# An earlier opening, rows of two, three and three sequences, and halved vector pieces in a two-layer gated attention kernel

## The chip, the cores and the metric

The kernel runs on one core of one Trainium2 chip. The metric is the device time of one execution in microseconds (us). The kernel before the change took 2823.27 us (median of 3 runs, 2820.88 to 2829.08).

## What is computed

The reference updates x (8 sequences of 512 tokens, 256 channels) four times, with a second input ctx (8 x 512 x 128) and a tanh gate before each update:

```python
x = x + tanh(g_xattn[0]) * L0_xattn(layernorm(x), ctx)   # 16 heads of 16: causal self plus cross attention
x = x + tanh(g_ffn[0])   * L0_ffn(layernorm(x))          # both linears on integers, scales taken over all of x
x = x + tanh(g_xattn[1]) * L1_xattn(layernorm(x), ctx)   # block a1 (self), then block a2 (cross), each attention + MLP
x = x + tanh(g_ffn[1])   * L1_ffn(layernorm(x))          # ternary linear, depthwise conv of 3, SiLU, ternary linear
```

The two scales of L0_ffn need the minimum and maximum over all sequences, so nothing behind them can start before the last sequence has passed. In layer 1 the blocks are per sequence: block a2 of a sequence needs the output of block a1 of the same sequence, and L1_ffn needs that of a2.

## The kernel before, in words

All work is cut into steps, and a planner in Python writes them out in one order when the program is built. The class `Pace` keeps, for each engine, the time at which it would be free, and for each tile the time at which it would be done. A step is a generator that stops at `need(...)` (L915), which names the tiles it waits for and whether its next instruction goes to TensorE. `weave_timed` (L1057) orders layer 0, `weave_all` (L1791) orders layer 1. Each picks, among the steps that could start within 0.3 us of TensorE's next free moment, the one with the lowest place in the plan: a stream's `base` plus its `share` of progress, against the index of the next attention step. A step that doesn't use TensorE is written out as soon as its tiles are ready. Streams with a `lag` (the lists of first and last jobs: 1.0) also wait until VectorE's planned queue is at most that long (L1808). The engines run what was written in that order, each waiting only for its data.

**Layer 0, opening (L1174).** The first sequence's normalisation (`norm0`), its transposes and self values (`pre0`), and its first query and key projections (`pairs0(0, 0, 0)`) are written alone, before the attention steps begin. PSUM has one bank (`m1`) for them, so each transpose group, each pair of value tiles and each projection waits until the one before has been copied out. The scores have three two-bank buffers (`st`), which are empty then. An attention step has a front (scores, exp on ScalarE, for self attention a causal mask on GpSimd) and a back (probabilities times values); a back is written one front later (`end_rest`).

**Layer 1 (L1757).** The order of the attentions is written by hand: slots 0 to 15, each one sequence and one block. The sequences go in rows of two: (0, a1), (1, a1), (0, a2), (1, a2), (2, a1), (3, a1), and so on. For every slot k there is a stream of projections (`pair1`), and one for each half of the MLP (`mlp1`, base k + 1). The MLP of block a1 goes on into `enter1`, which normalises twice and writes `zT`, from which the queries of the same sequence's a2 block are projected. The MLP weights are held for one block at a time and reloaded when a row ends. `first(b)`, the second linear of L0_ffn for sequence b, feeds block a1 of that sequence; `last(b)` is all of L1_ffn for it. These fifteen jobs stand in one list, `few`, sorted by base and worked off strictly one behind the other; `tail` does L1_ffn for sequence 7.

In `first`, each half of a sequence is one ScalarE operation and two VectorE operations over 2048 columns (L1912 to L1916). In `last`, each half has a maximum over 2048 columns (L2298), a product (L2313) and a rounding (L2315). The load of the a2 values into `vt` stands inside `mlp1` (L2109).

Of the kernel before, what the change touches and what calls it, by code (L numbers as in the profile page):

```python
# [25 lines left out]
MAGIC = 12582912.0  # L26
NEG = -1.0e30
PTS = 3
KEYS_FIRST = 6
# [884 lines left out]

def need(*tiles, pe=True, room=()):  # L915


    return [Pace.name(t) for t in tiles], pe, room

# [29 lines left out]
class Fast(General):  # L949
# [114 lines left out]
    def weave_timed(self, ops, streams, drain=False):  # L1064
# [17 lines left out]
        def starts(s):  # L1082
            names, on_pe, room = s.need
            t = max([pace.when(names)] + [pace.place(tag) for tag in room])
            return max(t, pace.place("m1")) if on_pe else t
# [73 lines left out]
    def layer0_xattn(self, w8pool):  # L1159
# [4 lines left out]
        with (  # L1164
# [8 lines left out]
            self.load0(wpool)  # L1173
            self.weave_timed([], [Stream(self.chain(self.norm0(0), self.pre0(0), self.pairs0(0, 0, 0)), 1.0)])  # L1174
            for b in range(B):
                streams = [Stream(self.pairs0(b, 1), 7.0, 0.88)]
                if b:
                    streams.append(Stream(self.post0(b - 1), 4.0, 0.88))
                else:
                    streams.insert(0, Stream(self.cross0(0), 5.0, 2.0))  # L1180
                if 1 <= b <= 4:
# [162 lines left out]
    def pre0(self, b):  # L1344
# [24 lines left out]

    def pairs0(self, b, u, *which):  # L1370

        work, q = self.work, self.seqs[b]

        while u and (0, 1) not in q:
            yield WAIT
        for s in which or (0, 1):
            src = (q["xnT"], q["ctxT"])[s]
            yield need(q["xnT"])
            ps = self.proj(self.wqk[("wq", "wcq")[s]], q["xnT"], u * P)
# [3 lines left out]
            ps = self.proj(self.wqk[("wk", "wck")[s]], src, u * P)  # L1383
            KT = [work.tile([P, T], F32, tag="KT", name="KT", bufs=8) for _ in range(2)]
            for e in range(2):
                self.out_of(KT[e], ps, self.par[:, e : e + 1], self.kbe[:, s, u, e : e + 1])
            q[u, s] = (QT, KT)

    def steps0(self, b, u):
# [7 lines left out]
        def front_at(e, s):  # L1397
            if (u, s) not in q or ("v", s) not in q:
                return 1e9
# [3 lines left out]
        def front(e, s, kt):  # L1403
# [9 lines left out]
            if s == 0:  # L1413
# [4 lines left out]
                )  # L1418
            reads = [Pace.name(pt), Pace.name(q["v", s])]
            self.coming = (reads, kt == 0, lambda: back(e, s, kt, lo, pt))  # L1420

# [35 lines left out]
        def rest_at():  # L1457
            if self.rest is None:
                return 0.0
            names, opens, _ = self.rest  # L1460
            t = pace.when(names)
# [275 lines left out]
    def layer1_xattn(self):  # L1737
        nc, tc = self.nc, self.tc
        with (
# [18 lines left out]
            self.li1s, self.mlps, self.loads, self.both_in = [0, 0], [0, 0], {}, {}  # L1758
            order = [(2 * p + k, blk) for p in range(B // 2) for blk in range(2) for k in range(2)]
# [16 lines left out]
            for half in range(2):  # L1776
                mlps[half][-1].base += 0.4 * half
                mlps[half].append(Stream(self.tail(half), 20.0, 1.0, 17 + 0.4 * half))
            self.final, self.tails = {}, [0, 0]
# [3 lines left out]
            self.weave_all(  # L1783
                [self.steps1(b, blk) for b, blk in order], [few, pairs, *mlps, *pres, diag, keys]
            )
# [5 lines left out]
    def weave_all(self, attns, chains):  # L1791
# [60 lines left out]
    def weight(self, name, b, blk):  # L1852

        while self.loads.get(name) != self.slot_of(b, blk) // 2:
# [30 lines left out]
    def first(self, b):  # L1885
# [142 lines left out]
    def slot_of(self, b, blk):  # L2028

        return 4 * (b // 2) + 2 * blk + b % 2  # L2030

# [8 lines left out]
    def pair1(self, b, blk, g):  # L2040
# [16 lines left out]
        q["QK", blk, g] = (QT, KT)  # L2057
        self.pairs += 1

    def mlp1(self, b, blk, half):  # L2060
# [38 lines left out]
        if blk:  # L2099
# [3 lines left out]
            nc.vector.scalar_tensor_tensor(res, res, self.gate[:, 1:2], x, ALU.mult, ALU.add)  # L2103
        elif not half:
            while self.nvt < self.slot_of(b, 1) or self.backs < 16 * (self.slot_of(b, 1) - 1):
                yield WAIT
            vt = q["vt", 1] = work.tile([P, NT, 2 * C], F32, tag="vt", name="vt", bufs=2)
            self.nvt += 1
            nc.sync.dma_start(vt.rearrange("p t c -> p (t c)"), self.vd[b])  # L2109
        li2 = yield from self.weight("li2", b, blk)  # L2110
# [133 lines left out]
    def last(self, b):  # L2244
# [25 lines left out]
        for half in range(2):  # L2270
# [3 lines left out]
            for f in range(NF):  # L2274
# [18 lines left out]
            yield need(h, pe=False)  # L2293
            nc.scalar.activation(h, h, AF.Silu)
            yield need(h, pe=False)

            hm = work.tile([P, n], F32, tag="hm", name="hm")
            nc.vector.tensor_reduce(  # L2298
                hm, h.rearrange("p f t -> p t f"), AX.X, ALU.max, apply_absolute_value=True
            )  # L2300
            yield need(hm)
# [9 lines left out]
            nc.scalar.copy(sr, self.row_of(sc, range(2)))  # L2311
            yield need(sr, pe=False)
            nc.vector.tensor_tensor(h, h, sr.unsqueeze(1).to_broadcast([P, NF, n]), ALU.mult)  # L2313
            hq = work.tile([P, NF, n], BF16, tag="hq", name="hq")
            nc.vector.tensor_scalar(hq, h, MAGIC, MAGIC, ALU.add, ALU.subtract)  # L2315
            nc.vector.tensor_scalar(k, un, self.units["f1_w2"], self.gate[:, 3:4], ALU.mult, ALU.mult)
# [238 lines left out]
```

## Time and profile before

| what | value |
|---|---|
| median of 3 runs | 2823.27 us |
| the profiled execution | 2823.82 us, span 2822.1 us |
| TensorE busy | 2520.0 us, 89% |
| VectorE, ScalarE, GpSimd busy | 61%, 51%, 22% |
| mean granted TensorE clock | 0.956 |
| first scores of layer 0 | 30.70 us |
| end of layer 0's attentions, about | 720 us |
| last instruction of layer 1's slots 0, 5, 10, 15 (copy of the last head group) | 1014.0, 1562.6, 2105.8, 2667.7 us |

A slot of layer 1 takes some 110 us: (2667.7 - 1014.0) / 15. PE is TensorE, PEld its weight loads, DVE VectorE, ACT ScalarE, POOL GpSimd. "PEclk" is the TensorE clock that was granted, as a share of full speed. In a timeline the columns are start, duration, engine, line, operation, output and input, and in brackets the idle time before it with what ended it. In a table of windows each engine has its busy time and, in brackets, its instructions; behind them stand the granted clock, the DMA share and GB/s.

### The profile page before, as it was taken

What the parts mean: (1) busy time and instruction counts of PE and PEld (TensorE: products, weight loads), DVE (VectorE), ACT (ScalarE), POOL (GpSimd) and SP (SyncE); (2) the same over time, 40 slices, a digit from 0 to 9 for tenths busy, and PEclk for the clock granted to TensorE, in tenths of its full rate; (3) what the DMA queues carried; (4) which work ended last, traced back from release to release, by engine and by line L of the source; (5) the groups of instructions that cost most, each with busy time, mean ns of one, the idle gap of its engine ahead of it and who ended that gap; (6) DMA issues with size and microseconds to landing.
All of it is one profiled execution on the core that took longest, in us unless ns stands there. A gap on an engine that the chain in (4) does not pass through costs nothing.

```text
span 2822.1 us, 38446 instructions
## 1 busy us (share of the span) xinstructions
PE 2520.0 (89%) x15452; PEld 1222.3 (43%) x15452; DVE 1725.1 (61%) x3072; ACT 1448.3 (51%) x1785; POOL 615.0 (22%) x682
## 2 busy tenths in 40 slices
PE   6999999999675888999999998999999999898875
PEld 2333333333232334535554445456354455354454
DVE  4544544343475555575657767766767755768766
ACT  4666675666573444445445534454555454555431
POOL 2112222111101343231422121232223112212010
PEclk9999999999897989999999999999999999999988
DMA  3001110010364411312210120131120020121010
GB/s 111 22 29 49 49 64 27 12 34 12 116 272 178 154 45 64 113 64 75 72 53 23 45 90 24 59 131 50 53 90 31 28 78 23 31 83 46 15 45 16
DMA packets 77339, 181.79 MB, mean 64 GB/s; under 512 B 7520, under 2 KB 36576, under 8 KB 69344
## 3 DMA queue, kind: packets, MB, share of 16 engines
q1 hardware_dynamic: 74768, 176.05, 17.9%
q8 instruction: 123, 2.02, 0.3%
q0 software_dynamic: 800, 2.62, 0.3%
q10 hardware_dynamic: 1584, 0.58, 0.1%
q14 instruction: 64, 0.52, 0.1%
HBM read 116.32 MB, written 62.91 MB: 64 GB/s over the span
## 4 chain that ended last, share of the span: by engine, by line
PE 69%; DVE 17%; ACT 7%; issue 3%; POOL 3%; DMA 1%; ACTq 0%; POOLq 0%; DVEq 0%
PE ps L1050 39%; PE ps_s L1050 16%; PE ov L1050 12%; DVE hext L1665 2%; PE ps L1053 2%; POOL dg L2179 1%; ACT pt L1412 1%; ACT pt L2175 1%; DVE hF L2290 1%; DVE hm L2298 1%; DVE acc L2204 1%; DVE mv L1936 1%; DVE acc L2206 1%; DVE rb L2222 1%; ACT hD L2122 1%
## 5 line engine op out<-in xcount | busy, mean ns | idle before, releaser
L2175 ACT ACTIVATE pt<-ps_s 128x1024 f32<-128x1024 f32 x512 | 496.3, 1021 | 443.5 <-PE ps_s L1050 357.1
L1050 PE MATMUL ps_s<-QT,KT 32*128 32x512 f32 (+3 forms) x4096 | 613.2, 610 | 29.0 <-ACT pt L2175 12.6
L1412 ACT ACTIVATE pt<-ps_s 128x1024 f32<-128x1024 f32 (+3 forms) x512 | 411.2, 862 | 197.4 <-PE ps_s L1050 190.9
L1050 PEld LDWEIGHTS ps_s<-QT,KT 32*128 32x128 f32 x4096 | 192.5, 185 | 365.2 <-issue 204.4
L2179 POOL TENSOR_SCALAR_AFFINE_SELECT dg<-pt 128x512 f32<-128x512 f32 x128 | 123.2, 964 | 651.6 <-ACT pt L2175 651.5
L1050 PE MATMUL ps<-li,hD 128*128 128x256 f32 x1024 | 238.8, 389 | 12.1 <-ACT hD L2122 12.1
L1050 PE MATMUL ps<-x3T,li 128*128 128x256 f32 x1024 | 244.0, 390 | 1.4 <-ACT x3T L2092 1.1
L1050 PE MATMUL ov<-pt,v 128*32 128x512 f32 (+3 forms) x2048 | 232.7, 525 | 13.9 <-POOL pt L1415 12.5
L1050 PE MATMUL ov<-pt,vt 128*32 128x512 f32 (+3 forms) x1792 | 204.9, 524 | 39.4 <-DVE oT L2224 33.2
L1050 PEld LDWEIGHTS ps<-li,hD 128*128 128x128 f32 x1024 | 193.4, 193 | 66.2 <-issue 17.6
L1050 PEld LDWEIGHTS ps<-x3T,li 128*128 128x128 f32 x1024 | 192.1, 194 | 55.3 <-issue 15.3
L1415 POOL TENSOR_SCALAR_AFFINE_SELECT pt<-pt 128x512 f32<-128x512 f32 x128 | 87.0, 681 | 477.4 <-ACT pt L1412 477.4
L1942 POOL TENSOR_SCALAR mv<-mv 128x2 f32<-128x2 f32 (+1 forms) x105 | 49.8, 475 | 630.8 <-DVE mv L1937 589.8
L2206 DVE TENSOR_TENSOR acc<-acc,pt 128x2048 f32<-128x2048 f32 x64 | 151.4, 2366 | 8.2 <-ACT pt L2175 7.2
L2204 DVE TENSOR_TENSOR acc<-pt 128x2048 f32<-128x2048 f32 x64 | 149.9, 2342 | 0.6 <-ACT pt L2175 0.6
L1437 DVE STREAM_TRANSPOSE ot<-ov 128x512 f32<-128x512 f32 x64 | 45.8, 716 | 156.3 <-PE ov L1050 156.3
L1050 PE MATMUL ps<-zT,a_wq 128*128 128x512 f32 x256 | 131.7, 640 | 6.1 <-DVE zT L2023 4.1
L2290 DVE SCALAR_TENSOR_TENSOR hF<-hp,cols,hF 128x256 f32<-128x256 f32 x224 | 113.1, 505 | 34.6 <-ACT hF L2281 28.1
L1050 PE MATMUL ps<-li,oT 128*128 128x256 f32 x512 | 128.0, 394 | 1.6 <-DVE oT L2224 1.1
L1050 PEld LDWEIGHTS ps<-li,oT 128*128 128x128 f32 x512 | 94.0, 193 | 44.5 <-issue 16.4
L1050 PEld LDWEIGHTS ov<-pt,v 128*32 128x32 f32 x2048 | 40.5, 107 | 168.0 <-issue 102.2
L1729 ACT ACTIVATE hD<-ps,cols 128x256 f32<-128x256 f32 x121 | 53.7, 472 | 108.8 <-PE ps L1050 72.9
(293 smaller groups left out, 3624.1 us busy)
## 6 DMA issues: line engine op xcount, KB each, us to landing
hd<-h SPq DMA_DIRECT2D x16, 1024.0 KB, 3.9
hF<-hd SPq DMA_DIRECT2D x16, 1024.0 KB, 6.7
li<-in_w_a_dram SPq DMA_DIRECT2D x16, 1024.0 KB, 5.0
fw<-q_f_w SPq DMA_DIRECT2D x22, 512.0 KB, 6.0
xF<-xd SPq DMA_DIRECT2D x22, 512.0 KB, 4.5
kd<-k SPq DMA_DIRECT2D x8, 1024.0 KB, 5.6
vd<-v SPq DMA_DIRECT2D x8, 1024.0 KB, 5.3
res<-rd SPq DMA_DIRECT2D x32, 256.0 KB, 2.7
```

The lines of the kernel that those rows point to most:

```text
L1050: self.nc.tensor.matmul(out, lhsT, rhs, start=start, stop=stop, skip_group_check=True)
L1053: self.nc.tensor.transpose(out, in_, self.ident)
L1412: nc.scalar.activation(pt[:, 2 * jp : 2 * jp + 2, lo:], pss[jp][:, :, lo:], AF.Exp)
L1415: nc.gpsimd.affine_select(out=diag, in_=diag, compare_op=ALU.is_ge, fill=0.0, base=0, pattern=[[0, 4], [1, P]], channel_multiplier=-1,)
L1665: nc.vector.tensor_reduce(e, hh, AX.X, op)
L1729: self.nc.scalar.activation(out, ps, AF.Identity, bias=bias)
L1942: nc.gpsimd.tensor_scalar(rstd, mv[:, :, 1], EPS, None, ALU.add)
L2175: nc.scalar.activation(pt[:, 2 * jp : 2 * jp + 2, :], pss[jp], AF.Exp)
L2179: nc.gpsimd.affine_select(out=dg, in_=pt[:, :, diag], compare_op=ALU.is_gt, fill=0.0, base=0, pattern=[[0, 4], [-1, P]], channel_multiplier=1,
L2204: nc.vector.tensor_tensor(st["acc"], st["pt"], pt, ALU.add)
L2206: nc.vector.tensor_tensor(st["acc"], st["acc"], pt, ALU.add)
L2290: nc.vector.scalar_tensor_tensor(a, hp[:, half + k : half + k + n], self.col("conv_w", 3 * f + k), a, ALU.mult, ALU.add)
```

## The change

**Opening.** `opening0` takes the place of `pre0` for the first sequence. Its eight transposes go into the two banks of one score buffer without a copy between them; ScalarE copies one bank out and VectorE the other. Query and key projections then use the two banks of a second score buffer. The self values come no longer before the first scores but as the head of the stream that holds the cross values, woven among the attention steps. A front needs no values any more, only a back does.

**Rows.** The attentions of layer 1 go in rows of two, three and three sequences. Slots 0 to 3 stay; then come (2, a1), (3, a1), (4, a1), (2, a2), (3, a2), (4, a2), (5, a1), (6, a1), (7, a1), (5, a2), (6, a2), (7, a2). The bases of the first and last jobs change with it, and the load of the a2 values gets a stream of its own. Weights are reloaded at five row ends instead of seven.

**Pieces.** The operations over 2048 columns in `first`, and the maximum, product and rounding in `last`, are cut in two, with a stop of the planner between them. A step can now name ScalarE as the engine whose queue its lag refers to.

```diff
+ROWS = ((0, 1), (2, 3, 4), (5, 6, 7))
+FIRST_AT = (-1, 0, 1, 2, 4, 5, 7, 9)
+LAST_AT = (6, 7, 8, 11, 12, 13, 15)
...
-            self.weave_timed([], [Stream(self.chain(self.norm0(0), self.pre0(0), self.pairs0(0, 0, 0)), 1.0)])
+            self.weave_timed([], [Stream(self.chain(self.norm0(0), self.opening0()), 1.0)])
...
-                    streams.insert(0, Stream(self.cross0(0), 5.0, 2.0))
+                    values = self.values0(0, 0, self.seqs[0]["xnT"], self.wv0["wv"], "bv")
+                    streams.insert(0, Stream(self.chain(values, self.cross0(0)), 12.0, 1.2))
...
+    def opening0(self):
+        q = self.seqs[0]
+        xnT = q["xnT"] = self.work.tile([P, 2, T], F32, tag="xnT", name="xnT", bufs=1)
+        yield need(q["z"], pe=False)
+        ps = self.st.tile([P, 2, T], F32, tag="st", name="ps_s")
+        for c in range(2):
+            for i in range(NT):
+                self.tp(ps[:, c, i * P : (i + 1) * P], q["z"][:, i, c * P : (c + 1) * P])
+        self.nc.scalar.copy(xnT[:, 0, :], ps[:, 0, :])
+        self.nc.vector.tensor_copy(xnT[:, 1, :], ps[:, 1, :])
+        yield from self.pairs0(0, 0, 0, two=True)
...
+            banks = self.st.tile([P, 2, T], F32, tag="st", name="ps_s") if two else None
+            ps = self.proj(self.wqk[("wq", "wcq")[s]], q["xnT"], u * P, ps=two and banks[:, 0, :] or None)
...
-            if (u, s) not in q or ("v", s) not in q:
+            if (u, s) not in q:
...
-            for k, b in zip((-1, 0, 1, 2, 3, 4, 7, 8), range(B)):
+            for k, b in zip(FIRST_AT, range(B)):
...
-            for k, b in zip((5, 6, 9, 10, 13, 14, 15), range(B - 1)):
+            for k, b in zip(LAST_AT, range(B - 1)):
...
-            names, on_pe, _ = s.need
-            t = max(pace.when(names), pace.free["DVE"] - s.lag)
+            names, on_pe, _, on = s.need
+            t = max(pace.when(names), pace.free[on] - s.lag)
...
-        if self.both(b, (name, blk)) and b % 2 and (b, blk) != (B - 1, 1):
+        if self.both(b, (name, blk)) and b == self.rows[self.row_at(b, blk)][1][-1] and (b, blk) != (B - 1, 1):
...
-            yield need(h, pe=False)
-            nc.scalar.activation(h, h, AF.Identity, scale=self.rh, bias=self.magic)
-            yield need(h, pe=False)
-            nc.vector.tensor_scalar(h, h, self.hlo, self.hhi, ALU.max, ALU.min)
+            for f in (slice(0, NF // 2), slice(NF // 2, NF)):
+                yield need(h, pe=False, on="Activation")
+                nc.scalar.activation(h[:, f, :], h[:, f, :], AF.Identity, scale=self.rh, bias=self.magic)
             hq = work.tile([P, NF, n], BF16, tag="hq", name="hq")
-            nc.vector.tensor_scalar(hq, h, MAGIC, None, ALU.subtract)
+            for f in (slice(0, NF // 2), slice(NF // 2, NF)):
+                yield need(h, pe=False)
+                nc.vector.tensor_scalar(h[:, f, :], h[:, f, :], self.hlo, self.hhi, ALU.max, ALU.min)
+                nc.vector.tensor_scalar(hq[:, f, :], h[:, f, :], MAGIC, None, ALU.subtract)
...
+    def values2(self, b):
+        at = self.slot_of(b, 1)
+        while self.nvt < at or self.backs < 16 * (at - 1) or not self.keys_done:
+            yield WAIT
+        vt = self.seqs[b]["vt", 1] = self.work.tile([P, NT, 2 * C], F32, tag="vt", name="vt", bufs=2)
+        self.nvt += 1
+        self.nc.sync.dma_start(vt.rearrange("p t c -> p (t c)"), self.vd[b])
...
-            nc.vector.tensor_reduce(
-                hm, h.rearrange("p f t -> p t f"), AX.X, ALU.max, apply_absolute_value=True
-            )
+            for i in range(2):
+                yield need(h, pe=False)
+                t2 = slice(i * P, (i + 1) * P)
+                nc.vector.tensor_reduce(
+                    hm[:, t2], h[:, :, t2].rearrange("p f t -> p t f"), AX.X, ALU.max, apply_absolute_value=True
+                )
...
-            nc.vector.tensor_tensor(h, h, sr.unsqueeze(1).to_broadcast([P, NF, n]), ALU.mult)
...
-            nc.vector.tensor_scalar(hq, h, MAGIC, MAGIC, ALU.add, ALU.subtract)
+            for f in (slice(0, NF // 2), slice(NF // 2, NF)):
+                yield need(sr, pe=False)
+                nc.vector.tensor_tensor(
+                    h[:, f, :], h[:, f, :], sr.unsqueeze(1).to_broadcast([P, NF // 2, n]), ALU.mult
+                )
+                nc.vector.tensor_scalar(hq[:, f, :], h[:, f, :], MAGIC, MAGIC, ALU.add, ALU.subtract)
```

More of the change, by code (lines that the diff above doesn't have):

```diff
@@ L912, with need @@
 WAIT = object()
-def need(*tiles, pe=True, room=()):
-    return [Pace.name(t) for t in tiles], pe, room
+def need(*tiles, pe=True, room=(), on="DVE"):
+    return [Pace.name(t) for t in tiles], pe, room, on
 class Stream:
@@ L1082, in starts @@
         def starts(s):
-            names, on_pe, room = s.need
+            names, on_pe, room, _ = s.need
             t = max([pace.when(names)] + [pace.place(tag) for tag in room])
@@ L1368, in ctx0, with pairs0 @@
         self.nc.sync.dma_start(self.cd[b], cT)
-    def pairs0(self, b, u, *which):
+    def pairs0(self, b, u, *which, two=False):
         work, q = self.work, self.seqs[b]
@@ L1378, in pairs0 @@
             yield need(q["xnT"])
-            ps = self.proj(self.wqk[("wq", "wcq")[s]], q["xnT"], u * P)
+            banks = self.st.tile([P, 2, T], F32, tag="st", name="ps_s") if two else None
+            ps = self.proj(self.wqk[("wq", "wcq")[s]], q["xnT"], u * P, ps=two and banks[:, 0, :] or None)
             QT = work.tile([P, T], F32, tag="QT", name="QT", bufs=4)
@@ L1382, in pairs0 @@
             yield need(src)
-            ps = self.proj(self.wqk[("wk", "wck")[s]], src, u * P)
+            ps = self.proj(self.wqk[("wk", "wck")[s]], src, u * P, ps=two and banks[:, 1, :] or None)
             KT = [work.tile([P, T], F32, tag="KT", name="KT", bufs=8) for _ in range(2)]
@@ L1418, in front @@
                 )
-            reads = [Pace.name(pt), Pace.name(q["v", s])]
-            self.coming = (reads, kt == 0, lambda: back(e, s, kt, lo, pt))
+            reads = [Pace.name(pt), Pace.name(self.vts[s][b % 2])]
+            self.coming = (reads, kt == 0, lambda: back(e, s, kt, lo, pt), lambda: ("v", s) in q)
         def back(e, s, kt, lo, pt):
@@ L1459, in rest_at @@
                 return 0.0
-            names, opens, _ = self.rest
+            names, opens, _, there = self.rest
+            if not there():
+                return 1e9
             t = pace.when(names)
@@ L1758, in layer1_xattn @@
             self.li1s, self.mlps, self.loads, self.both_in = [0, 0], [0, 0], {}, {}
-            order = [(2 * p + k, blk) for p in range(B // 2) for blk in range(2) for k in range(2)]
+            self.rows = [(blk, bs) for bs in ROWS for blk in range(2)]
+            order = self.order = [(b, blk) for blk, bs in self.rows for b in bs]
             few, pairs, mlps, pres = [], [], [[], []], [[], []]
-            for k, b in zip((-1, 0, 1, 2, 3, 4, 7, 8), range(B)):
+            for k, b in zip(FIRST_AT, range(B)):
                 few.append(Stream(self.first(b), 3.8, 0.8, k, 1.0))
@@ L1778, in layer1_xattn @@
                 mlps[half].append(Stream(self.tail(half), 20.0, 1.0, 17 + 0.4 * half))
+            vals = [Stream(self.values2(b), 1.0) for b, blk in order if blk]
             self.final, self.tails = {}, [0, 0]
@@ L1783, in layer1_xattn @@
             self.weave_all(
-                [self.steps1(b, blk) for b, blk in order], [few, pairs, *mlps, *pres, diag, keys]
+                [self.steps1(b, blk) for b, blk in order], [few, pairs, *mlps, *pres, vals, diag, keys]
             )
@@ L1852, in weight @@
     def weight(self, name, b, blk):
-        while self.loads.get(name) != self.slot_of(b, blk) // 2:
+        while self.loads.get(name) != self.row_at(b, blk):
             yield WAIT
@@ L2028, in slot_of, with row_at @@
     def slot_of(self, b, blk):
-        return 4 * (b // 2) + 2 * blk + b % 2
+        return self.order.index((b, blk))
+    def row_at(self, b, blk):
+        return next(i for i, (k, bs) in enumerate(self.rows) if k == blk and b in bs)
     def turned_half(self, z):
@@ L2103, in mlp1 @@
             nc.vector.scalar_tensor_tensor(res, res, self.gate[:, 1:2], x, ALU.mult, ALU.add)
[L2104 to L2109, printed above, removed]
         li2 = yield from self.weight("li2", b, blk)
@@ L2292, in last @@
                     )
-            yield need(h, pe=False)
+            yield need(h, pe=False, on="Activation")
             nc.scalar.activation(h, h, AF.Silu)
-            yield need(h, pe=False)
             hm = work.tile([P, n], F32, tag="hm", name="hm")
-            nc.vector.tensor_reduce(
-                hm, h.rearrange("p f t -> p t f"), AX.X, ALU.max, apply_absolute_value=True
-            )
+            for i in range(2):
[4 more added lines that the diff above has]
+                )
             yield need(hm)
@@ L2311, in last @@
             nc.scalar.copy(sr, self.row_of(sc, range(2)))
-            yield need(sr, pe=False)
-            nc.vector.tensor_tensor(h, h, sr.unsqueeze(1).to_broadcast([P, NF, n]), ALU.mult)
             hq = work.tile([P, NF, n], BF16, tag="hq", name="hq")
-            nc.vector.tensor_scalar(hq, h, MAGIC, MAGIC, ALU.add, ALU.subtract)
+            for f in (slice(0, NF // 2), slice(NF // 2, NF)):
[4 more added lines that the diff above has]
+                nc.vector.tensor_scalar(hq[:, f, :], h[:, f, :], MAGIC, MAGIC, ALU.add, ALU.subtract)
             nc.vector.tensor_scalar(k, un, self.units["f1_w2"], self.gate[:, 3:4], ALU.mult, ALU.mult)
```

## The prediction

> **What bounds the kernel now.** First the busy times and slices of the page, then a table of windows by stage, then the waits of TensorE, then the timeline of the opening and of one stall.
>
> ```profile
> PE 2520.0 (89%) x15452; PEld 1222.3 (43%) x15452; DVE 1725.1 (61%) x3072; ACT 1448.3 (51%) x1785; POOL 615.0 (22%) x682
> ...
> PE   6999999999675888999999998999999999898875
> ...
> PEclk9999999999897989999999999999999999999988
> ```
>
> TensorE is the bound nearly everywhere. There are about 302 us in which it is idle (2822.1 - 2520.0), and they lie in the first slice, in slices 11 to 16 and in the last four. The table says more exactly where.
>
> ```profile
> 13.50:30.70 17.20, 12.55 (x32) 6.76 (x32) 7.15 (x19) 3.30 (x7) 5.44 (x3) 1.00 0.50 150
> 30.70:50.00 19.30, 15.35 (x98) 6.06 (x102) 9.64 (x33) 10.88 (x17) 7.32 (x9) 1.00 0.19 69
> 50.00:720.00 670.00, 653.07 (x4628) 234.97 (x4622) 298.91 (x627) 433.97 (x547) 125.30 (x170) 1.00 0.10 33
> 720.00:905.00 185.00, 115.51 (x413) 53.32 (x410) 119.33 (x142) 99.49 (x151) 15.11 (x20) 0.82 0.51 200
> 1135.00:2660.00 1525.00, 1415.22 (x8549) 747.17 (x8551) 1043.24 (x1784) 747.61 (x870) 357.07 (x369) 0.97 0.17 59
> 2660.00:2822.00 162.00, 107.34 (x502) 79.94 (x494) 105.82 (x210) 45.79 (x77) 12.27 (x19) 0.84 0.08 27
> ...
> 2530.00:2595.00 65.00, 53.74 (x302) 21.67 (x302) 48.94 (x100) 29.48 (x46) 19.20 (x20) 0.89 0.21 68
> ```
>
> Layer 0's attentions (50 to 720) are full: 98%. So what the opening saves arrives almost whole at 720 us. The stretch from 720 to 905 is the first linear of L0_ffn, which the change does not touch. In layer 1's body (1135 to 2660) TensorE is idle for 109.8 us, and the clock of 0.97 takes about 46 us more (1525 x 0.03); the two overlap. After 2660 it is idle for 54.7 us at a clock of 0.84.
>
> ```profile
> PE ov L1050 <- DVE oT L2224: 33.2, 22, 4.9
> ...
> PE ps L1053 <- DVE hm L2298: 16.7, 6, 6.5
> ...
> PE ps L1050 <- DVE hq L2315: 10.0, 6, 3.7
> ```
>
> These are TensorE's waits that the pieces aim at (total, times, longest): the next head group waits until VectorE has emptied the output bank, and `last` waits for its own long VectorE operations.
>
> **1. Opening.** The rows of before:
>
> ```profile
> 16.13 1.11 PE L1053 MATMUL ps<-ident,z 128*128 128x128 f32 x4 [0.68 <-ACT xnT L1319]
> ...
> 17.92 3.57 PE L1050 MATMUL ps<-wv_t,xnT 128*128 128x256 f32 x8 [0.67 <-ACT xnT L1319]
> ...
> 22.27 1.99 PE L1050 MATMUL ps<-wv_t,xnT 128*128 128x256 f32 x8 [0.78 <-DVE v L1336]
> ...
> 27.81 1.98 PE L1050 MATMUL ps<-xnT,wk_p 128*128 128x512 f32 x4 [0.78 <-ACT QT L1313]
> ...
> 30.70 0.71 PE L1050 MATMUL ps_s<-QT,KT 32*128 32x512 f32 x4 [0.90 <-DVE KT L1315]
> ```
>
> Each group waits 0.7 to 0.8 us for the one bank. After the change the second transposes follow the first at 15.5 and end near 16.6. The second half of `xnT` is copied by VectorE, which is an added wait: it queues behind the packing of the weights and the small bias operations, the last of which runs from 18.07 to 18.41 (`gbp`). A VectorE copy of 128x512 out of PSUM takes 0.68 us (row of `zT`, L2023), so `xnT` is whole at 19.1 instead of 17.87. The query projection (1.98) can do its first chunk before that, so it ends at 20.1 to 21.1; the key projection (1.98) follows without a wait and ends at 22.1 to 23.1; one copy to `KT` (0.81) and the first scores start at 22.9 to 23.9. If the projections start as slowly as the first values did (3.57 against 1.99), it is 25.5. That is 5.2 to 7.8 us before 30.70. The values (2 x 1.99 us, with 0.69 us of VectorE after each, in one bank) then come before the first back. They fill the time in which TensorE waited for the first exponentials, where it was idle for 3.95 us (30.7 to 50); what does not fit there comes off the gain. I take **-5 us**. The ends: all idle time after 13.5, 4.65 + 3.95 = -8.6; and +1, if values and late copy cost more than the waits.
>
> **2. Rows.** In rows of two, the second sequence's a2 slot comes right after the slot in which its a1 MLP runs. The MLP of slot 13 writes its last result at 2532, `zT` follows, and the first query of slot 15 is copied at 2557.6, 4 us after slot 14's last head group (2553.4). Slot 11 is late likewise (2107.2 against 2105.8), slot 7 leads by 6 us only (1660.5 against 1666.7), while slots 4, 5, 6 and 14 lead by 22 to 24. Around these three places (1640 to 1710, 2085 to 2155, 2530 to 2595) TensorE is idle for 9.8, 7.4 and 11.3 us, and clocks of 0.93, 0.98 and 0.89 take 4.9, 1.4 and 7.2. Together 42 us in 205; at the body's mean rates (7.2% and 3%) it would be 21. The excess is 21 us. In rows of three there is a whole slot more between the two, so this lateness should go. What is late next is the head group's own copy, as everywhere. I take **-18 us**, bounds -25 (two more transitions of this kind a little better) and 0.
>
> The moved load of the a2 values (one DMA of 0.43 us on SP's queue, at 1455.0 for slot 6, issued about a slot ahead) and six weight loads fewer (two row ends, three tiles each) cost or save nothing: no TensorE wait names them, and the DMA share is 0.17.
>
> The clock in this stretch deserves a look, since idle time costs twice. From 1462 to 1465 TensorE was busy 0.71 us, and from 1465 to 1471 the granted clock was 0.50. The Trainium skill ("TensorE: Matmul & The Clock Gate", Part 1) has the rate halved only after a whole idle window of about 3.4 us. By that rule only three waits of this body (4.89, 4.06 and 4.04 us) could lose clock and the gain here would be some 5 us smaller; the row shows a loss after a shorter wait, so I count the clock as measured.
>
> **3. Pieces.** One operation becomes two: 32 + 14 + 28 = 74 more on VectorE (`first` 16 halves, `last` 14) and 16 more on ScalarE. A tensor-tensor takes 0.69 us on 512 columns and 2.29 on 2048, so each has about 0.16 us that does not shrink: 12 us of VectorE. In the body VectorE is 68% busy; the cover is there, but not inside a chain of its own. What it brings: the chain that empties the output bank no longer stands behind a whole 3.71 us maximum or 2.29 + 1.23 us product and rounding. But not every stall has that cause: of the two longest, the one at 2590.06 (4.06 us) stood behind a normalisation that took 2.69 us for two operations while GpSimd was busy, and the one at 1204.12 (4.89 us) behind such a one and an addition of 2.79. The three waits above sum to 59.9 us; I take a sixth, **-10 us**, bounds -25 and +6 (half of the added 12).
>
> **4. The end.** The fifteen first and last jobs are one serial list. The outputs of `last` left at 1628.88, 1807.15, 2104.87, 2276.66, 2523.50, 2686.64 and 2795.10: a job takes 160 to 190 us beside attentions, 108 alone. In the new order sequence 5's a2 is slot 13 instead of 11, so `last(5)` can start only near slot 15 (now 14.7), and more of it is left when the attentions end. VectorE is 65% busy there. I take **+6 us**, bounds -5 and +55.
>
> **Sum.** -5 - 18 - 10 + 6 = -27. From the profiled execution's own 2823.82 that is 2796.8, so **2797 us**; the median of the runs (2823.27) is 0.5 us lower, which changes nothing.
>
> **Rivals.**
>
> *A. The list of jobs is late (slower).* `first(4)`, `first(5)` and `last(0)` now stand one slot later, and `first(7)` stands behind `last(2)`, which cannot start before slot 8's MLP is done. At 1.6 slots per `last` and 0.45 per `first`, counted from 5.5, `first(7)` is done at 5.5 + 3 x 1.6 + 2 x 0.45 = 11.2 to 11.6, and slot 12 wants its queries at 11.8. Then all of the list ends up to a slot (110 us) later; at the end, where a job takes 108 us instead of 175, half of that is left: +55 instead of +6, and 2823.8 - 33 + 55 = **2846 us**. For it: the list was busy without a break from 1392 to 2795, only 27 us before the end. Against it: jobs that are overdue have the lowest place and are picked first. It decides once the last output of sequence 5 leaves over 50 us after the last head group (19 us now).
>
> *B. The idle time only moves (same).* The planner fills what it can; late queries give way to other waits for VectorE, and the 18 us and half of the 10 are not seen: 2823.8 - 5 - 5 + 6 = **2820 us**. For it: slot 3 is also a second sequence and has little idle time (1.9 us in 1215 to 1270), so rows of two need not stall.
>
> *C. More than the sum.* If half of the body's 110 us of idle time goes and the clock with it (23), 2823.8 - 78 + 6 is about **2752 us**. For it: only that the lateness is spread; against it: VectorE's load stays.
>
> *D. The opening does nothing,* because the late copy eats it: +5 on the forecast, 2802, inside its range.
>
> **Chances.** The forecast with D: 0.56 (its own range 2775 to 2814). C: 0.07. B: 0.14. A: 0.23. A measurement of this kernel tells differences over about 0.3% (8.5 us) from none. Faster is the forecast and C, 0.63; within 0.3% is B, 0.14; slower is A, 0.23. A range of 2762 to 2846 leaves out most of C and the upper half of A, under 0.2.
>
> **What would show it.** Right: first scores near 24 us instead of 30.70 and layer 0's end some 5 us earlier; first queries of slots 7, 8, 9, 13, 14 and 15 about 20 us ahead of the slot before; idle time of layer 1's body under 95 us with a clock above 0.97; the wait for `oT` below 33 us; from the last head group to the end about 160 us (154 now). Wrong: a gap before slot 12 with TensorE waiting for `zT` or the first queries, an end over 200 us after the last head group, or more idle time around the pieces in which VectorE works through them one by one.

## The result, and the profile after

The changed kernel takes 2794.64 us (median of 4 runs, 2792.5 to 2797.81) beside 2823.33 us for the kernel before (4 runs): a ratio of 0.9896 [0.9878, 0.9914]. The profiled execution took 2795.52 us, span 2793.8. The forecast was 2797.

The busy times, the slices of TensorE and its granted clock on the page of the kernel after:

```profile
PE 2515.3 (90%) x15447; PEld 1220.4 (44%) x15452; DVE 1734.5 (62%) x3128; ACT 1457.3 (52%) x1813; POOL 615.9 (22%) x682
...
PE   7999999999774989999999989998999989999875
...
PEclk9999999999987999999999999999999999999987
```

TensorE's work is the same. The clock still dips between the layers (slices 12 and 13 now) and at the end; the dip of before in slice 15, about the end of slot 0, is gone. The table of windows by stage, with the borders moved to about the stages of this kernel:

```profile
13.50:28.00 14.50, 12.61 (x26) 5.60 (x26) 7.64 (x21) 3.54 (x7) 5.79 (x3) 1.00 0.59 178
28.00:50.00 22.00, 19.39 (x121) 8.00 (x121) 11.13 (x35) 11.80 (x17) 7.36 (x9) 1.00 0.00 1
...
716.00:900.00 184.00, 116.63 (x415) 52.87 (x417) 120.11 (x145) 101.31 (x154) 13.55 (x20) 0.82 0.50 198
1130.00:2632.00 1502.00, 1408.20 (x8592) 745.55 (x8585) 1045.88 (x1808) 756.64 (x899) 365.57 (x369) 0.98 0.17 56
2632.00:2793.80 161.80, 107.03 (x462) 79.53 (x460) 108.38 (x225) 41.43 (x65) 11.66 (x19) 0.79 0.08 27
```

The body of layer 1 has 93.8 us of idle time (1502.0 - 1408.20) at a clock of 0.98, where it had 109.8 at 0.97. The end has a somewhat lower clock. The figures of 0.79 and 0.84 can't be set side by side, since this table's last border lies 2.7 us behind the last head group and that of before lay 7.7 us ahead of it; with the border at the last head group in both, the clock of the end is 0.80 against 0.83. TensorE's waits that the pieces aimed at, and three others (total, times, longest), of the kernel after:

```profile
PE ov L1053 <- DVE oT L2257: 26.6, 19, 3.0
PE ps_s L1053 <- ACT pt L2208: 25.0, 31, 3.0
PE ps L1056 <- DVE z L144: 17.5, 15, 3.0
...
PE ps L1056 <- DVE hm L2333: 9.9, 6, 3.2
PE ov L1053 <- POOL dg L2212: 9.6, 10, 3.4
...
PE ps L1053 <- DVE hq L2353: 5.8, 5, 2.0
```

The three others in the kernel before:

```profile
PE ov L1050 <- POOL dg L2179: 19.1, 13, 5.6
...
PE ps L1053 <- DVE z L141: 12.9, 13, 2.4
PE ps_s L1050 <- ACT pt L2175: 12.6, 25, 1.3
```

The three waits for `oT`, `hm` and `hq` fell from 59.9 to 42.3 us, the one for `dg` from 19.1 to 9.6. The one for the normalisations' `z` rose from 12.9 to 17.5, and the one for ScalarE's exponentials (`pt` of L2208, L2175 before) doubled, from 12.6 to 25.0.

The copy of the last head group of each slot cuts the span into three parts: up to the end of slot 0; the body, slots 1 to 15; and the end. In the body, "idle" is TensorE's idle time and "clock" is what the granted clock takes (length x (1 - clock)), summed slot by slot. All in us:

| kernel | end of slot 0 | body | idle | clock | end |
|---|---|---|---|---|---|
| before | 1014.0 | 1653.7 | 123.0 | 52.3 | 154.4 |
| after | 1003.9 | 1625.5 | 106.1 | 35.8 | 164.5 |
| opening alone | 1010.2 | 1657.0 | 122.7 | 57.1 | 154.6 |
| rows and places alone | 1014.9 | 1618.8 | 101.9 | 37.8 | 169.9 |
| pieces alone | 1005.0 | 1657.5 | 111.8 | 65.6 | 159.1 |
| after, both lists of places old | 1004.2 | 1670.0 | 129.4 | 58.2 | 164.9 |
| before, both lists of places new | 1014.3 | 1680.5 | 144.8 | 65.9 | 168.7 |

So the 28.3 us of span are -10.1 up to slot 0, -28.2 in the body and +10.1 at the end. Body length less idle and clock is 1478 us before and 1484 after, and between 1470 and 1482 in the other five: what differs is nearly all idle time and lost clock. Each row is one profiled execution. Two further kernels with the same opening and pieces, and with the first four places as in the kernel after, ended slot 0 at 998.6 and 1000.7, so some 5 us of the first column are not told from the spread of executions. "Places" are the bases of the first and last jobs, `FIRST_AT` and `LAST_AT`.

### The profile page after: what moved, and what is told of

The parts are those of the page before. It is cut to its first block, busy times and chain, and to the rows that moved or that the text cites. A ratio compares the mean times of both kernels' runs of the same rounds, so it can differ in the third digit from the quotient of the medians.

```text
span 2793.8 us, 38496 instructions
## 1 busy us (share of the span) xinstructions
PE 2515.3 (90%) x15447; PEld 1220.4 (44%) x15452; DVE 1734.5 (62%) x3128; ACT 1457.3 (52%) x1813; POOL 615.9 (22%) x682
## 4 chain that ended last, share of the span: by engine, by line
PE 68%; DVE 18%; ACT 7%; POOL 3%; issue 3%; DMA 1%; ACTq 0%; POOLq 0%; DVEq 0%; SPq 0%
PE ps L1053 39%; PE ps_s L1053 16%; PE ov L1053 12%; DVE hext L1686 2%; ACT pt L2208 2%; PE ps L1056 2%; DVE hF L2323 1%; ACT pt L1431 1%; DVE acc L2237 1%; POOL dg L2212 1%; DVE mv L1962 1%; DVE rb L2255 1%; DVE rt L2252 1%; DVE hm L2333 1%; DVE oT L2257 1%
## 5 line engine op out<-in xcount | busy, mean ns | idle before, releaser
L2208 ACT ACTIVATE pt<-ps_s 128x1024 f32<-128x1024 f32 x512 | 496.2, 1021 | 427.8 <-PE ps_s L1053 320.2
L1053 PE MATMUL ov<-pt,vt 128*32 128x512 f32 (+3 forms) x1792 | 203.3, 524 | 33.4 <-DVE oT L2257 26.6
L2212 POOL TENSOR_SCALAR_AFFINE_SELECT dg<-pt 128x512 f32<-128x512 f32 x128 | 114.0, 891 | 520.9 <-ACT pt L2208 520.8
L1968 POOL TENSOR_SCALAR mv<-mv 128x2 f32<-128x2 f32 (+1 forms) x105 | 60.0, 572 | 754.0 <-DVE mv L1963 719.9
```

Source lines behind the costliest of these rows:

```text
L1053: self.nc.tensor.matmul(out, lhsT, rhs, start=start, stop=stop, skip_group_check=True)
L1968: nc.gpsimd.tensor_scalar(rstd, mv[:, :, 1], EPS, None, ALU.add)
L2208: nc.scalar.activation(pt[:, 2 * jp : 2 * jp + 2, :], pss[jp], AF.Exp)
L2212: nc.gpsimd.affine_select(out=dg, in_=pt[:, :, diag], compare_op=ALU.is_gt, fill=0.0, base=0, pattern=[[0, 4], [-1, P]], channel_multiplier=1,
```

## The experiments

**The parts by themselves.** Three kernels have one part of the change each, one has rows and pieces without the opening. The edits are the parts of the diff above; the rows' part has the places and the stream for the a2 values with it.

> The kernel before with the new opening alone. In the profile of the changed kernel the first scores came at 27.99 us, only 2.7 us earlier, and the loads behind layer 0's end 1.5 us earlier (873.08 against 874.54). Theory (the sum on record, opening mis-sized): 1 to 3 us less than before, some 2821, ratio 0.999 to 1.000. Rival (the opening did bring its 5 us, and the rest of layer 0 lost part of it by another order): 5 us less or more, ratio 0.998 or lower.

> The kernel before with rows of two, three and three alone, with their bases and the moved load, without the new opening and the shorter pieces. Theory (late second sequences are the largest term): 15 to 22 us less than before, some 2805, ratio 0.992 to 0.995, and the first queries of every slot from 4 on lead the end of the slot before by 20 us or more. Rival (the pieces bring most, the rows little): ratio above 0.997.

> The kernel before with the shorter pieces and the lag on ScalarE alone; rows of two and the old opening. Theory: 5 to 12 us less than before, some 2815, ratio 0.996 to 0.998; the wait for the output bank falls below 33 us. Rival (pieces carry the gain): 18 us or more less, ratio below 0.994. Second rival (the pieces cost what they bring): ratio 0.999 to 1.001.

> The changed kernel with the old opening: rows and pieces together. Theory: 26 us less than before, some 2797, ratio 0.990 to 0.992, and it differs from the sum of rows alone and pieces alone by less than 5 us. Rival (the parts help or hinder each other): it differs from their sum by 8 us or more.

| kernel | median us | ratio to before, 95% |
|---|---|---|
| opening alone | 2822.39 | 0.9988 [0.9979, 0.9997] |
| rows and places alone | 2802.71 | 0.9919 [0.9907, 0.9932] |
| pieces alone | 2825.07 | 0.9997 [0.9987, 1.0008] |
| rows, places and pieces | 2798.62 | 0.9902 [0.9887, 0.9916] |

The kernel before took 2825.82 us beside these four: -3.4, -23.1, -0.8, and -27.2 for rows with pieces. The gain is that of the rows and places. The pieces are worth nothing alone; beside the rows they measure 4.1 us, which the intervals (0.9902 and 0.9919, each within 0.0015) don't tell from nothing.

**The opening's clock.** The projections of the kernel after did not take the time of the rows of before. TensorE's timeline of the kernel after:

```profile
13.57 2.80 PE L1056 MATMUL ps_s<-ident,z 128*128 128x128 f32 x8 [13.57 <-ACT z L1974]
17.24 4.24 PE L1053 MATMUL ps_s<-xnT,wq_p 128*128 128x512 f32 x4 [0.86 <-DVE wq_p L1236]
22.26 3.78 PE L1053 MATMUL ps_s<-xnT,wk_p 128*128 128x512 f32 x4 [0.78 <-ACT QT L1317]
25.83 2.23 PE L1053 MATMUL ps<-wv_t,xnT 128*128 128x256 f32 x8
27.99 1.14 PE L1053 MATMUL ps_s<-QT,KT 32*128 32x512 f32 x8
```

4.24 and 3.78 us stand where 1.98 each were counted, and the key projection waits 0.78 us for the copy of `QT`, though it writes the other bank of that buffer. The granted clock of this stretch reads 1.00, and yet one matmul takes twice its usual time: the rows of the query weights `wq_p`, with minimum, median and maximum in ns, have

```profile
L1053 PE MATMUL ps<-xnT,wq_p x60: 592/592/697, 44.3 to 648.4; 128*128 128x512 f32 x60
...
L1053 PE MATMUL ps_s<-xnT,wq_p x4: 1057/1126/1222, 17.2 to 20.4; 128*128 128x512 f32 x4
```

for the 60 later ones and the first four. Two kernels put transposes of the identity, whose result nothing reads, into a buffer of their own ahead of the first real ones: 40 in the one, 64 and 8 more between the real ones and the projections in the other, where queries and keys also get two separate buffers.

```diff
+        warm = self.st.tile([P, 2, T], F32, tag="st", name="ps_s")
+        for i in range(40):
+            self.tp(warm[:, i % 2, (i // 2 % NT) * P : (i // 2 % NT + 1) * P], self.ident)
         yield need(q["z"], pe=False)
```

> The changed kernel with 40 transposes of the identity into a free score buffer while TensorE has nothing to do before the first normalisation is ready; nothing reads them. In the changed kernel the first query and key projections took 4.24 and 3.78 us instead of 1.98 each. Theory (TensorE came to them after 13 us of idleness and ran at half rate, which ate the opening's gain): both take 2.0 to 2.8 us, the first scores come 2.5 to 4 us before 27.99, and the whole takes 2 to 4 us less than the changed kernel (ratio to the kernel before 0.988 to 0.9895). Rival (the projections are slow because of where they write or because of the copy of xnT): they stay at 3.7 us or more and the time doesn't change.

> The changed kernel with 64 transposes of the identity up to the first real ones, 8 more behind those, and one score buffer each for queries and keys. With 40 of them TensorE stood idle for 3 us before the first real transposes, the granted clock fell to 0.50 from 16.7 us on, and the projections stayed slow. Theory (clock): the clock stays at 1.00 from 10 us on, both projections take 2.0 to 2.4 us, the keys no longer wait 0.78 us for the copy of the queries, the first scores come at 23 to 24 us instead of 27.99, and the whole is 3 to 5 us shorter than the changed kernel. Rival (the opening's gain is lost again in layer 0, as the 2.7 us at the first scores became 1.5 to 4 at its end): first scores at 24, time within 1.5 us of the changed kernel.

With 40, the first of them, up to 6.8 us, took 421 ns each (median) and those behind them 273, so TensorE became faster some 3.7 us after it began (3.13), while the granted clock reads 1.00 throughout. The table of windows says what the clock did behind that:

```profile
7.00:10.50 3.50, 3.34 (x24) 3.10 (x22) 0.87 (x4) 0.20 (x1) 0.58 (x2) 1.00 0.97 368
10.50:13.40 2.90, 0.03 (x1) 0.04 (x1) 2.12 (x3) 0.69 (x2) 2.90 (x3) 1.00 0.49 89
13.40:16.70 3.30, 1.81 (x8) 0.90 (x8) 3.30 (x4) 1.97 (x4) 3.10 (x2) 0.80 0.90 307
16.70:25.00 8.30, 7.31 (x8) 2.52 (x9) 2.20 (x13) 0.69 (x1) 2.34 (x1) 0.50 0.36 104
```

The 40 were through at 10.34; TensorE was idle for 3.03 us and then had only eight transposes, the first three of them singly with gaps. From about 15.4 (0.80 over this window, if it fell once from 1.00 to 0.50) to 25 the clock was 0.50, and the projections took 4.24 and 3.78 us as without the 40. A clock of 0.50 is thus what such a projection takes. With 64 and 8, and with buffers of their own, the timeline reads

```profile
16.56 1.10 PE L1053 MATMUL ps_s<-xnT,wq_p 128*128 128x512 f32 x2
18.73 1.12 PE L1053 MATMUL ps_s<-xnT,wq_p 128*128 128x512 f32 x2 [1.07 <-DVE xnT L1371]
19.69 1.88 PE L1053 MATMUL ps_s<-xnT,wk_p 128*128 128x512 f32 x4
21.41 1.89 PE L1053 MATMUL ps<-wv_t,xnT 128*128 128x256 f32 x8
23.23 1.14 PE L1053 MATMUL ps_s<-QT,KT 32*128 32x512 f32 x8
```

Full rate, no wait for the copy of `QT`, and first scores at 23.23, in the place the forecast gave (22.9 to 23.9), with the 1.07 us for VectorE's late copy that it counted. Of the 4.8 us between 27.99 and 23.23, some 0.7 came in because VectorE had packed the query weights earlier in this execution (the first projection starts at 16.56 instead of 17.24). The other 4.1 are nearly all half clock and the shared buffer together; one kernel put both right at once, so their shares were not measured apart. Layer 0's last output `ot` was transposed 4.3 us earlier (722.5 against 726.8) and slot 0 ended 7.9 us earlier (996.0 against 1003.9); at slot 15 4.5 were left. Only part of this is the opening: in four other kernels with the opening of the kernel after, `ot` came between 724.8 and 726.8 and slot 0 ended between 998.6 and 1004.2. The medians are 2797.73 us, 0.9909 [0.9887, 0.9931], with 40, and 2793.27 us, 0.989 [0.9875, 0.9905], with 64 and 8, beside 0.9896 for the kernel after: what the second one saves in the opening can't be told from nothing in the time. That is what the rival of its expectation foretold (within 1.5 us of the changed kernel).

**Late second sequences, or something else.** My reason for the rows was that the first queries of slots 7, 11 and 15 come late. The next kernels move that lateness by other means: rows of three, three and two; the new rows with both old lists of places; and rows of two in which the MLP of block a1 gets a lower `share`, so that it runs sooner.

```diff
-ROWS = ((0, 1), (2, 3, 4), (5, 6, 7))
-FIRST_AT = (-1, 0, 1, 2, 4, 5, 7, 9)
+ROWS = ((0, 1, 2), (3, 4, 5), (6, 7))
+FIRST_AT = (-1, 0, 1, 3, 4, 5, 8, 9)
```

> The changed kernel with rows of three, three and two (first jobs at -1, 0, 1, 3, 4, 5, 8, 9). Theory: sequence 5's last job starts two slots earlier, so the end behind the last head group shrinks from 164 us to 155 or less, but slots 3 of the first row no longer and the last slot again are second sequences of a short row: the first queries of slot 15 lead by less than 5 us instead of 21. The two about cancel: within 6 us of the changed kernel, ratio to before 0.9875 to 0.992. Rival (the end is set by the order of the tail alone, whatever the rows): the end stays at 162 us or more and the time rises by 6 us or more.

```diff
-FIRST_AT = (-1, 0, 1, 2, 4, 5, 7, 9)
-LAST_AT = (6, 7, 8, 11, 12, 13, 15)
+FIRST_AT = (-1, 0, 1, 2, 3, 4, 7, 8)
+LAST_AT = (5, 6, 9, 10, 13, 14, 15)
```

> The changed kernel with the old bases of the first and last jobs (first at -1, 0, 1, 2, 3, 4, 7, 8; last at 5, 6, 9, 10, 13, 14, 15). Theory (the list of jobs is served late because it begins a slot later): the first output of last leaves 50 us or more before 1719, the end behind the last head group shrinks by 5 us or more, and the time falls by 3 to 8 us. Rival (the list is paced by VectorE's queue, and what it does early is taken from the attentions): the end shrinks, the attentions end later by as much, and the time stays within 3 us of the changed kernel.

The third is an edit of the kernel before:

```diff
-                    mlps[half].append(Stream(self.mlp1(b, blk, half), 20.5, 0.88 if blk else 0.5, k + 1))
+                    mlps[half].append(Stream(self.mlp1(b, blk, half), 20.5, 0.88 if blk else 0.25, k + 1))
```

> The kernel before, rows of two, with one number changed: the share of block a1's MLP streams 0.25 instead of 0.5, so that they go ahead of the attention steps sooner. Theory (the late second sequences cost some 20 us): the first queries of slots 7, 11 and 15 lead by 10 us or more (6, -1 and -4 before) and the time falls by 5 to 12 us, ratio 0.996 to 0.998. Rival (lateness of the queries costs nothing by itself; rows of three help by spreading the work): the leads rise and the time stays, ratio 0.999 to 1.001. Second rival: the MLP is bound by its own chain, and the leads do not rise.

How far the first queries of a slot are ahead of the last head group before it, in us, and the time:

| kernel | slot 7 | slot 11 | slot 15 | median us | ratio, 95% |
|---|---|---|---|---|---|
| before | 6.2 | -1.4 | -4.2 | | 1 |
| after | 20.0 | 23.0 | 21.0 | 2794.64 | 0.9896 [0.9878, 0.9914] |
| rows and places alone | 24.8 | 24.5 | 20.4 | 2802.71 | 0.9919 [0.9907, 0.9932] |
| after, both lists old | 24.1 | 26.7 | 21.3 | 2839.05 | 1.0045 [1.003, 1.0059] |
| before, a1 MLPs sooner | 14.6 | 7.8 | 14.7 | 2837.45 | 1.0051 [1.0034, 1.0068] |
| before, both lists new (below) | 23.7 | 8.9 | 9.4 | 2871.18 | 1.0161 [1.0147, 1.0175] |
| after, rows of three, three, two | 23.8 | 21.0 | 9.4 | 2811.74 | 0.995 [0.9931, 0.9968] |

As an account of the whole time the theory falls. With the old places in the new rows every lateness is cured and the kernel is 44 us slower than the changed one, which neither expectation allowed; with the a1 MLPs sooner in rows of two no first query is late any more, and 12 us are lost (2837.45 - 2825.29). Rows of three, three and two are slower than the changed kernel too, and their end is no shorter (164.1 us), as the rival had it: the order (0, 1, 2) first is not the better one with these places.

At the three places themselves the theory holds. The prediction measured three stretches about the ends of slots 6, 10 and 14 of the kernel before (70, 70 and 65 us, one line of them shown there). The other two, and then the stretches as far from the ends of the same slots in the kernel after:

```profile
1640.00:1710.00 70.00, 60.20 (x309) 27.43 (x307) 55.82 (x117) 29.27 (x41) 25.58 (x30) 0.93 0.18 61
2085.00:2155.00 70.00, 62.58 (x342) 28.78 (x338) 51.69 (x110) 29.18 (x42) 25.38 (x26) 0.98 0.30 102
```

```profile
1626.70:1696.70 70.00, 66.35 (x411) 32.07 (x412) 53.68 (x84) 35.33 (x43) 16.14 (x15) 0.95 0.16 53
2076.90:2146.90 70.00, 64.91 (x470) 34.33 (x463) 50.93 (x78) 36.51 (x46) 26.63 (x28) 1.00 0.27 91
2510.20:2575.20 65.00, 60.76 (x361) 26.63 (x360) 47.41 (x86) 35.06 (x54) 10.10 (x10) 1.00 0.21 65
```

Idle time and clock of the three stretches together, and of the rest of the body, in us:

| kernel | three stretches | rest of the body |
|---|---|---|
| before | 41.9 | 133.4 |
| after | 16.5 | 125.4 |
| after, both lists old | 21.7 | 165.9 |
| before, a1 MLPs sooner | 30.7 | 153.7 |
| before, both lists new | 29.2 | 181.5 |

Wherever the lateness goes, the stretches lose 11 to 25 us of idle time and clock. But the rest of the body changes with it, by -8 to +48 us, and that decides the time. The stretches are the same by slot number; in the new rows other sequences' work stands in them.

**Places against rows.** The other corner of the square is the kernel before with nothing but the new places; two more put back one list each in the changed kernel.

```diff
-            for k, b in zip((-1, 0, 1, 2, 3, 4, 7, 8), range(B)):
+            for k, b in zip((-1, 0, 1, 2, 4, 5, 7, 9), range(B)):
...
-            for k, b in zip((5, 6, 9, 10, 13, 14, 15), range(B - 1)):
+            for k, b in zip((6, 7, 8, 11, 12, 13, 15), range(B - 1)):
```

> The kernel before, rows of two, with only the bases of the first and last jobs changed to the new ones. With rows of three and the old bases the time was 0.45% above before, and earlier MLPs in rows of two, which cured the late queries, cost 0.5%: so late second sequences are not what the 18 us stood for. Theory (the new bases bring most of it by spreading the jobs' VectorE work): 12 us or more less than before, ratio 0.9955 or lower. Rival (rows and bases only work together: later jobs need the later slots of rows of three): ratio 0.998 or higher.

The changed kernel with the old last jobs' places only:

```diff
-LAST_AT = (6, 7, 8, 11, 12, 13, 15)
+LAST_AT = (5, 6, 9, 10, 13, 14, 15)
```

> The changed kernel with the old bases of the last jobs only (5, 6, 9, 10, 13, 14, 15); the first jobs keep the new ones. Rows of three with both old cost 44 us against the changed kernel. Theory (it is the place of last(2) and first(7) among the others that fills slots 10 and 11, and that comes from the last jobs' bases): 25 us or more above the changed kernel, ratio to before above 0.999. Rival (the first jobs, which in the old bases ran a slot earlier and crowded slots 3 to 6): within 12 us of the changed kernel, ratio below 0.994.

The changed kernel with the old first jobs' places only:

```diff
-FIRST_AT = (-1, 0, 1, 2, 4, 5, 7, 9)
+FIRST_AT = (-1, 0, 1, 2, 3, 4, 7, 8)
```

> The changed kernel with only the places of the eight first jobs put back, (-1, 0, 1, 2, 3, 4, 7, 8); the last jobs keep their new places, (6, 7, 8, 11, 12, 13, 15). With both lists old the ratio to the kernel before was 1.0045, with only the last jobs' places old 0.996, with both new 0.9896. Theory 1, each list has its own price and the two add: the first jobs' places were worth 1.0045 - 0.996 = 0.0085, so this kernel comes out near 0.9896 + 0.0085 = 0.998, some 24 us slower than the changed kernel, with more idle time in slots 8 to 12, where first(5) to first(7) then come earlier. Theory 2, the price is that of crowding: an early first job hurts only where an early last job stands beside it, so that here, with the last jobs late, there is room and the time stays within 0.3% of the changed kernel (0.987 to 0.993). First(7) stands before last(2) in either list; a time over 1.002 would mean that the place of the first jobs decides alone.

| rows | both lists old | last old | first old | both new |
|---|---|---|---|---|
| of two (kernel before) | 1 | | | 1.0161 [1.0147, 1.0175] |
| two, three, three (with opening and pieces) | 1.0045 [1.003, 1.0059] | 0.996 [0.9945, 0.9976] | 0.9929 [0.9915, 0.9943] | 0.9896 [0.9878, 0.9914] |

Neither the rows nor the places gain anything alone: the new places cost 1.6% in the old rows, and the new rows with old places, opening and pieces are 0.45% slower than the kernel before. Only together do they gain. Each list put back costs by itself 0.3 to 0.6%, and both together 1.5%: more than the sum, so my theory of two separate prices (0.998 for the old first jobs' places) falls. Crowding of the two lists, which allowed up to 0.993, is borne out by the median alone; its interval reaches 0.9943. The old last jobs' places alone, 0.996, lie between the two expectations for them (above 0.999, below 0.994) and fit neither.

Where the badly placed jobs show is in single slots. Slots 10 and 11 with both old lists, and then of the kernel after:

```profile
2006.70:2135.50 128.80, 113.40 (x714) 62.81 (x715) 90.58 (x164) 57.70 (x71) 32.84 (x37) 0.96 0.18 62
2135.50:2267.40 131.90, 115.99 (x711) 63.74 (x710) 96.90 (x162) 59.96 (x71) 32.77 (x36) 0.92 0.09 31
```

```profile
1981.80:2097.70 115.90, 106.63 (x705) 59.20 (x704) 86.57 (x137) 61.25 (x73) 20.58 (x24) 0.99 0.17 57
2097.70:2217.00 119.30, 110.15 (x713) 60.53 (x712) 92.77 (x177) 59.45 (x72) 46.09 (x51) 0.99 0.18 59
```

VectorE has 187.5 us to do in these two slots against 179.4, and TensorE is idle for 31.3 us against 18.4 at a clock of 0.96 and 0.92 against 0.99. TensorE's own work in them is larger too, 229.4 us against 216.8. But VectorE's load is not the whole measure: slots 9 to 12 of the kernel after have more VectorE work (349 us) than those with the old lists (336) and lose less. Which pairs of jobs collide was not settled.

One thing holds in the profiles of 12 kernels, all but the one with 40 transposes and the last one, though it was found after the runs and no kernel tests it. The slot with the last a1 attention of a row loses 15 to 19 us in idle time and clock on average, the other slots of the body 7.5 to 12. Rows of two have four such slots (71.9 us before), the new ones three (47.7). One fewer, at the difference of 8.6 us before (18.0 - 9.4), explains a quarter of the 33.4 us by which the body's idle time and clock fell.

## Why the prediction was right, and where it was not

**The opening: mechanism right, size wrong, by two steps.** "The query projection (1.98)", "the key projection (1.98) follows without a wait": the measured terms are 4.24, a wait of 0.78, and 3.78. First scores came at 27.99, outside even the 25.5 given for a slow start, which slowed one projection and not both. Most of the error lies in the choice of row: I took the 1.98 from rows that ran after 25 us, while these matmuls run before it. The row that was nearest in time, the first values at 17.92 with 3.57 us for work that later took 1.99, was the right one for both. The second step is the order: "The values ... then come before the first back" counts them behind the first scores, but eight of their matmuls were written ahead of these. `KT`'s first copy was done at 26.95, and the scores waited another 1.0 us until TensorE was through with the values (25.83 to 28.06). The Trainium skill ("TensorE: Matmul & The Clock Gate", Part 1) calls the half rate the default until TensorE has been busy for a window of some 3.4 us; the 40 transposes agree on the default, since those of the first 3.7 us took 421 ns each and the later ones 273. On the way back no idle window of that length was needed: 3.03 us of idle time and a few sparse transposes were enough for half rate. Alone the opening saves 3.4 us (0.9988 [0.9979, 0.9997]) instead of 5. Layer 0's last `ot` came 1.4 us earlier (726.8 against 728.2), not 5.

**The rows: size about right, reason incomplete.** "The excess is 21 us. ... this lateness should go." It did go, and the three stretches lost 25.4 us of idle time and clock (41.9 to 16.5). The step that failed is the one from there to the time, which took the rest of the body as unchanged: three kernels without the lateness are slower than the one with it, because they lose 20 to 48 us more in the rest. -18 for the rows and +6 for the end make -12; the rows with their places measure -23.1, in the profiles -34.9 in the body and +15.5 at the end. What I left out is that the change is of three tables that belong together. I counted the new `FIRST_AT` and `LAST_AT` only as a risk (rival A), where the runs show that there is no gain without them: with the old ones the body has 1670.0 us instead of 1625.5. That the sum came near is in part luck.

**The pieces: waits right, gain wrong.** The waits for `oT`, `hm` and `hq` fell as foretold, and VectorE's work rose about as foretold (13.8 us for the pieces alone, 12 reckoned). What the sum left out is that other waits grow: the one for ScalarE's `pt` is 26.8 us with the pieces alone and 25.0 in the kernel after, against 12.6 before, 12.3 with the opening alone and 16.5 with the rows. Why the pieces lengthen it was not tried. Alone, the pieces end slot 0 9.0 us earlier (1005.0 against 1014.0). Some 4 us of that are the chain of `first(0)`, whose matmuls start at 885.33 instead of 889.65; the rest was not followed. They give it all back: +3.8 in the body, where 11.2 us less idle time stand against 13.3 us more lost clock, and +4.7 at the end. That makes -0.8 us alone and -4.1 beside the rows, instead of -10. This is rival B, for this part only.

**The end: right in sign, a little short.** +10.1 instead of +6. The output of sequence 5 in the kernel before, and in the kernel after:

```profile
2686.64 0.39 SPq L2326 DMA_DIRECT2D out_dram<-xF  x1
```

```profile
2668.22 0.39 SPq L2364 DMA_DIRECT2D out_dram<-xF  x1
```

It leaves 38.9 us after the last head group (2629.3) instead of 19.0. Rival A was to decide from 50 on: the list is later, and not late enough. There was no gap before slot 12 either, whose first queries lead by 24.7 us. With the old places the first output of the list leaves at 1621.0 instead of 1719.6, and the end is no shorter (164.9), so the length of the end is not bought by an earlier start of the list.

**The sum** of -27 came true (-28.7 by the medians) with terms that were off by up to 11 us and partly cancelled: 1.6 too much for the opening, 6 to 9 too much for the pieces, 11 too little for rows and end together. Of the signs named, those of the body (idle time under 95 us, clock above 0.97), of the wait for `oT`, of the first queries (20.0 to 33.3 us ahead in slots 7, 8, 9, 13, 14 and 15) and of the end near 160 us came in; those of the opening did not. The signs of the first queries also come in in kernels that are slower than the one before: a sign that a slower kernel shows as well does not prove the account of the gain.

## What to carry to other kernels

In a kernel whose order is written by a planner, the order of the main work and the places of the filler work are one parameter: price them together, and try them together, since each alone may be worse than nothing. Curing a wait that can be named in the profile can bring what it cost at its place and lose more elsewhere: read the whole stage, and cure the wait by other means too, before giving it the gain. For matmuls that move to the start of a program, take durations from rows at that point of the timeline, not from the same instruction later.

## What the hardware showed that was not expected

- The granted clock reads 1.00 in the first 25 us of the kernels before and after, while TensorE ran at about half rate there: in the kernel before in the first values (3.57 us against 1.99), in the kernel after in the projections (1126 ns a matmul against 592, weight loads 310 against 190). In the kernel with 40 more transposes, whose projections took exactly as long, the same stretch reads 0.50. So a 1.00 at the start of a profile need not be measured; the durations of the instructions tell the rate.
- From half rate back to full took long: at 0.50 from 16.70 to 25.00, TensorE was busy for 7.31 of 8.30 us.
- A VectorE normalisation of 128x256 (`z`) took 381 to 1425 ns in the kernel after. Its median for `xo` was 413 ns before, 572 after, 1010 with both old lists in the new rows, and 569 in the slowest kernel, that of the new places in the old rows; so it does not follow the time. What shares a resource with it there was not tried.
- The kernel with the old first jobs' places spread over 16 us (2790.61 to 2806.58 in 6 runs) and the one with the pieces alone over 18 (2811.59 to 2829.69 in 12), the changed one over 5 (4 runs). The profiled execution of the first of these was its fastest, so no stage is explained from its profile here.
